# A decoder layer on one core: biases and beta added by accumulating transfers, the context's products in other accumulators, one product order, and the expert rows in another pool

## The chip, the cores and the metric

The kernel runs on one core of a Trainium2 chip. The metric is the device time of one execution in microseconds (us), lower being better. The core has five engines with a queue each, worked off in order: PE (TensorE, the matmuls; its weight loads, PEld, overlap them), DVE (VectorE), ACT (ScalarE), POOL (GpSimd) and SP (SyncE, which here only issues transfers). Transfers are issued from SP, ACT or POOL and share 16 DMA engines.

## What is computed

A decoder layer in float32, for x of 2 x 512 tokens by 1024 (E), that is 8 tiles of 128 tokens, and a context of 2 x 1024 by 1024:

```python
x = _layernorm(x + _L0_attn_ref(x, Wq, bq, Wk, bk, Wv, bv))       # per token, over head dims
x = _layernorm(x + _L0_xattn_ref(x, ctx, ...))                    # fake-quantised x @ fake-quantised ctx
x = _layernorm(x + _L0_ffn_ref(x, gate_w, up_w, down_w, fc1_w, fc2_w, expert_w, gamma, beta))
```

In the attention a token attends among its own 32 head dimensions: q (32 x 32), k and v (32 x 8) are projections with biases bq, bk, bv; the scores are a 32 x 32 matrix per token. The last part is relu(x up)^2 down, plus (x fc1) times the sum of the two largest gate logits, times expert and fc2, under a layer norm with gamma and beta.

## The kernel before

**Tiles and blocks.** Two tiles make a block of 256 tokens; there are four blocks. The tiles' own work is the generator `token_path` (L571): attention on DVE (`scores` L393, `exponentials` L412, `attend` L420), then the product with the quantised context (`cross` L527), then the hand-over (`hand_over` L617: transposes of the tile for the feed-forward, and `xc += beta` on POOL, L623, for the residual that is added at the very end, L774). The feed-forward of a block is the generator `ffn` (L649): 16 products with `up` (L695, PE name pu), 4 with `fc1` (pl), then `down` (L795, block 0, PE name pd) or `down_seven` (L851, blocks 1 to 3, PE name ps), which makes a product of 2 x 2 pieces with seven products in place of eight: per group of rows it needs sums of the activations (`unit_sums` L826) and of the weights (`weight_sums` L839, DVE L846 to L848).

**Order.** A loop at the end (L926 to L956) draws steps from the generators so that tiles of block n+1 are worked beside the feed-forward of block n. Before block 0, the generator `fill` (L334) runs beside tiles 0 and 1: it projects tiles 2 to 7 to q, k, v (L147, L152), copies them by ACT (L180, L181) and stores them to `qkv_d` in device memory from ACT's queue (L185, L186); then it multiplies expert and fc2 into four row blocks `e2` (L384, copies L388, stores L390 from POOL). The framework orders the instructions of each engine by an estimate of its own as it builds the program, within the dependencies; `tc.issue_after(i)` holds an instruction behind `i`.

**Biases.** bq (summed over four heads), bk and bv are spread to all partitions by a matmul and kept in `bqkv` (L213). Tiles 0 and 1 get the bias for q and k as they leave PSUM (L178). Later tiles are fetched back by `fetch_qkv` (L168, POOL's queue, L170 and L171) and get it on DVE (L189). The bias of v is added on DVE for every tile (L193).

**PSUM.** `ps_mm` has 2 banks (tag mm), for pu, pl, the context's products py (L559, L562) and pe; `ps_dn` has 4 (tag dn), for the projections and for pd and ps; `ps_tr` has 2. A py is taken out by DVE (L566), a pu by ACT (L722), a pl by DVE (L736).

**Seven products.** `order` (L883) is the order of the seven products of a group: (1, 2, 3, 6, 7, 5, 4), or (1, 6, 7, 5, 4, 2, 3) where the last three groups of the last block run together. Four banks hold them: 1 and 6, 2 and 3, 7 and 5, and 4. Products 1, 2, 3 read loaded weights as they are, 6 reads a sum that L847 writes over a part of them, 7 and 5 sums of L846, 4 a sum of L848. After the last group of each half (n = 0, 1) the banks are taken out: ACT L904 (1), DVE L905 (6), L906 (7), L907 and L908 (5), L909 (4), L912 (2 and 3). The weights come by `down_rows` (L753), 1 MB each, in three buffers (two of tag wb, one of tag wc).

**Pools.** `front` (L96) holds the projection weights, the x tiles (tag xs) and their transposes; the expert rows also take its xs buffers (L379). It is closed at L940, and the pools h, ffn, sums and more are opened in its place: the up activations, the relu buffers, the weight sums (and the loads of the second context, L477), one weight buffer. `work` has 3 buffers of 128 x 1024 for several short-lived rows.

Of the kernel before, what the change touches and what calls it, by code (L numbers as in the profile page):

```python
# [9 lines left out]
F32 = mybir.dt.float32  # L10
BF16 = mybir.dt.bfloat16
AF = mybir.ActivationFunctionType
ALU = mybir.AluOpType
# [3 lines left out]
P = 128  # L17
# [10 lines left out]
def kernel(  # L28
# [24 lines left out]
    nc = tc.nc  # L53

    B, S, E = x.shape
    _, D, H = wq.shape
    G = wk.shape[2]
    J = H // G
    DG = D * G
# [9 lines left out]
    TB = 2  # L69
    NB = TB * P  # L70
    NBLK = NT // TB
    HALF = 512
    DC = 8
# [39 lines left out]


    wqkv = [frontp.tile([P, 3 * DG], F32, name=f"wqkv_{k}") for k in range(KE)]
    bqkv = const.tile([P, 3 * DG], F32, name="bqkv")
    wq2 = wq.rearrange("e d h -> e (d h)")
    wk2 = wk.rearrange("e d h -> e (d h)")
    wv2 = wv.rearrange("e d h -> e (d h)")
# [54 lines left out]
    def projected(t, pqk, pv):  # L174

        qk, v = new_qkv(t, t >= TB)
        if t < TB:
            nc.vector.tensor_add(qk, pqk, bqkv[:, 0 : 2 * DG])  # L178
        else:
            nc.scalar.copy(qk, pqk)  # L180
        nc.scalar.copy(v.rearrange("p g e -> p e g"), pv[:, :DG].rearrange("p (e g) -> p e g", g=G))  # L181
        if t < TB:
            qkv[t] = qk, v
        else:
            nc.scalar.dma_start(qkv_d[t, :, 0 : 2 * DG], qk)  # L185
            nc.scalar.dma_start(qkv_d[t, :, 2 * DG :], v.rearrange("p g e -> p (g e)"))  # L186

    def bias_qk(qk):
        nc.vector.tensor_add(qk, qk, bqkv[:, 0 : 2 * DG])  # L189

    def bias_v(v):
        ve = v.rearrange("p g e -> p e g")
        nc.vector.tensor_add(  # L193
            ve, ve, bqkv[:, 2 * DG : 3 * DG].rearrange("p (e g) -> p e g", g=G)
        )


    brow = attp.tile([P, E], F32, tag="s", name="brow", bufs=2)
# [9 lines left out]
    for lo, n in ((0, 2 * DG), (2 * DG, DG)):  # L208
        pb = ps_mm.tile([P, HALF], F32, tag="mm", name=f"pb_{lo}")
        nc.tensor.matmul(  # L210
            pb[:, :n], ones_row[0:1, :], bqk_row[0:1, lo : lo + n], start=True, stop=True
        )
        nc.scalar.copy(bqkv[:, lo : lo + n], pb[:, :n])  # L213

# [62 lines left out]
    beta = const.tile([P, E], F32, name="beta")  # L277
# [55 lines left out]

    def fill():  # L334
        aside = context_tiles(0)
        xT = load_xT(TB)
        for t in range(TB, NT):
            for _ in range(2):
                next(aside, None)
            if t == NT - 3:  # L340
                nc.sync.dma_start(gamma, ln_gamma.partition_broadcast(P))
                nc.sync.dma_start(beta, ln_beta.partition_broadcast(P))
            ps = projection_psum(t)
            following = None
            for k in range(KE):
                project_qk(ps[0], xT, k)
                project_v(ps[1], xT, k)
                if k == 3:
                    yield 5.2
                if k == 4 and t + 1 < NT:  # L350

                    following = load_xT(t + 1)
                    yield 1.3
            xT = following
            projected(t, *ps)
            yield 5.2
        ex = wstream.tile([P, NL, LAT], F32, tag="wa", name="ex")
        nc.sync.dma_start(ex, expert_w.rearrange("(k p) n -> p k n", p=P))
        fc2 = []
        for c in range(NL // 2):  # L360
            w = wstream.tile([P, 2, E], F32, tag="wb", name=f"fc2_{c}")
            nc.sync.dma_start(w, fc2_w.rearrange("(k p) n -> p k n", p=P)[:, 2 * c : 2 * c + 2, :])
            fc2.append(w)
        expert = [None]
        exT = wstream.tile([P, NL, LAT], F32, tag="wa", name="exT")
        for m in range(NL):
            pt = ps_tr.tile([P, NL, P], F32, tag="tr", name=f"pt_ex_{m}")
            for l in range(NL):
                nc.tensor.transpose(pt[:, l, :], ex[:, l, ts(m, P)], ident)
            nc.scalar.copy(exT[:, m, :], pt.rearrange("p a b -> p (a b)"))  # L370
        yield 2.6
        for l in range(NL):

            while l >= NL // 2 and 1 not in crossed:
                yield 1.0
            if l == NL // 2:
                with tc.issue_after(expert[0].ins):
                    held.pop()()
            row = frontp.tile([P, E], F32, tag="xs", name=f"e2_{l}", bufs=2)  # L379
            for n in range(2):  # L380
                ps = ps_mm.tile([P, HALF], F32, tag="mm", name=f"pe2_{l}_{n}")
                with tc.issue_after(crossed[1].ins) if l >= NL // 2 else ExitStack():
                    for m in range(NL):
                        expert[0] = nc.tensor.matmul(  # L384
                            ps, exT[:, m, ts(l, P)], fc2[m // 2][:, m % 2, ts(n, HALF)],
                            start=(m == 0), stop=(m == NL - 1),
                        )
                nc.scalar.copy(row[:, ts(n, HALF)], ps)  # L388
                yield 3.5
            nc.gpsimd.dma_start(e2[ts(l, P), :], row)  # L390


    def scores(t, qk):  # L393
        q3 = qk[:, 0:DG].rearrange("p (d g) -> p d g", g=G)
        k3 = qk[:, DG : 2 * DG].rearrange("p (e g) -> p e g", g=G)
        s = attp.tile([P, D, D], F32, tag="s", name=f"s_{t}", bufs=2)
        for c in range(D // DC):
            prod = attp.tile([P, DC * D * G], F32, tag="prod", name=f"pqk_{t}_{c}", bufs=2)
            nc.vector.tensor_tensor(  # L399
                prod.rearrange("p (d e g) -> p d e g", d=DC, g=G),  # L400
                q3[:, ts(c, DC), :].unsqueeze(2).to_broadcast([P, DC, D, G]),
                k3.unsqueeze(1).to_broadcast([P, DC, D, G]),
                ALU.mult,
            )
# [122 lines left out]
    def cross(t, xc, cq, crow):  # L527
# [28 lines left out]
        nc.vector.tensor_mul(r, total, s12d2)  # L556
        nc.vector.scalar_tensor_tensor(xc, xc, r, crow, ALU.add, ALU.add)
        for h in range(E // HALF):
            py = ps_mm.tile([P, HALF], F32, tag="mm", name=f"py_{t}_{h}")  # L559
            with behind_products():  # L560
                for k in range(KC):
                    crossed[t] = nc.tensor.matmul(  # L562
                        py, aT[:, k, :], cq[:, k, ts(h, HALF)], start=(k == 0), stop=(k == KC - 1)
                    )
            xh = xc[:, ts(h, HALF)]
            nc.vector.scalar_tensor_tensor(xh, py, ns12, xh, ALU.mult, ALU.add)  # L566
# [4 lines left out]
    def token_path():  # L571
# [3 lines left out]
        for blk in range(NBLK):  # L575
            xcs = []
            x2T = []
            for i in range(TB):
# [5 lines left out]
                    fetch_qkv(t + 1)  # L584
                if t == TB:
                    first = last
                if t >= TB:

                    with tc.issue_after(first.ins):
                        bias_qk(qk)  # L590
                if ahead is None:
                    ahead = scores(t, qk)
                while True:
                    try:
                        step = next(ahead)
# [2 lines left out]
                        break  # L598
                    yield step
                exponentials(t, s)  # L600
                with tc.issue_after(first.ins) if t >= TB else ExitStack():
                    bias_v(v)
                yield 3.1
                ahead = None
                if t == 0:
# [11 lines left out]
                def hand_over(blk=blk, t=t, i=i, xc=xc, x2T=x2T):  # L617
                    if not x2T:
                        x2T.append(attp.tile([P, KE, NB], F32, tag="x2T", name=f"x2T_{blk}"))
                    with behind_products():  # L620
                        transpose_f32(x2T[0][:, :, ts(i, P)], xc, f"x2_{t}")

                    nc.gpsimd.tensor_tensor(xc, xc, beta, ALU.add)  # L623

# [226 lines left out]
    def down_seven(blk, h, units):  # L851
# [17 lines left out]
        while g < len(groups):  # L869
# [5 lines left out]
            if j == 0:  # L875
# [3 lines left out]
                    for i in range(4)  # L879
                ]  # L880
                banks = {1: b[0][:, 0], 6: b[0][:, 1], 2: b[1][:, 0], 3: b[1][:, 1],
                         7: b[2][:, 0], 5: b[2][:, 1], 4: b[3][:, 0]}
            order = (1, 6, 7, 5, 4, 2, 3) if along > 1 else (1, 2, 3, 6, 7, 5, 4)  # L883
            for m in order:
                for gg in range(g, g + along):
                    jj = groups[gg][1]
                    for k in range(2):
                        begins = jj == 0 and k == 0
                        second = begins and m in FIRST_OF

                        behind = began[FIRST_OF[m]] if second else above
                        with tc.issue_after(behind.ins) if begins else ExitStack():
                            began[m] = lately[0] = nc.tensor.matmul(  # L893
                                banks[m], units[jj][m][:, k, :], weights[gg][m][:, k, :],
                                start=begins and not second,
                                stop=(jj == len(h) - 1 and k == 1 and m not in FIRST_OF.values()),
                            )
# [92 lines left out]
```

## Time and profile before

| | |
|---|---|
| Median of 3 runs | 740.75 us (740.57, 740.75, 743.47) |
| The profiled execution's own time | 743.63 us |
| Its span, first to last instruction | 741.9 us |
| Mean granted TensorE clock | 0.989 |
| PE busy | 712.4 us (96%) |
| DVE busy | 576.4 us (78%) |
| ACT, POOL busy | 190.3 us (26%), 78.6 us (11%) |
| DMA | 122.70 MB, mean 165 GB/s |
| xc += beta on POOL (L623) | 8 x 2886 ns |
| bias adds on DVE (L189, L193) | 6 x 678 ns, 8 x 599 ns |

How to read it: busy time is the sum of an engine's instructions. The matmuls are pipelined, so a PE that shows busy may still start the next one late; the spacing of starts tells more. A row of the groups gives line, engine, operation, what is written from what, the shapes and the count, then busy time and mean of one, then the engine's idle time just before and what ended it. A row of the timeline gives start and length in us, engine, line, operation, and in brackets the idle time before it and what ended that. A table by stretches gives for each engine the busy time and, in brackets, its number of instructions, then the granted clock of PE, the busy share of the DMA engines and their GB/s.

### The profile page before, as it was taken

To read this page: it belongs to the slowest core of one execution; us is meant where nothing else is said; L and a number is where in the kernel's file an instruction comes from. 1 tells how busy PE (TensorE), PEld (TensorE's weight loads), DVE (VectorE), ACT (ScalarE), POOL (GpSimd) and SP (SyncE) were. 2 spreads that over 40 slices of the span, in tenths; PEclk is the share of its full clock that TensorE was granted. 3 is DMA by queue.
4 is the path that set the end of the run, shared out by engine and by line. 5 is a ranking of instruction groups with operands and counts; after the bars stand their busy time and mean duration, and the time that the engine had idled before them with its cause. 6 is when DMAs were issued, how large, how long until landed. Compare 5 with 4: busy or idle time off the path is not lost.

```text
span 741.9 us, 7731 instructions
## 1 busy us (share of the span) xinstructions
PE 712.4 (96%) x3076; PEld 537.8 (72%) x3076; DVE 576.4 (78%) x660; ACT 190.3 (26%) x308; POOL 78.6 (11%) x84
## 2 busy tenths in 40 slices
PE   6999999989999999999899999999999999999993
PEld 3666554468876444687688778887888888888882
DVE  4699997799999999999989999995437492013636
ACT  2097322222361214365140001243100012200001
POOL 2000002310101103120001020210100110000001
PEclk9999999999999999999899999999999999999997
DMA  7988103195535446574336444753554445445401
GB/s 277 346 308 318 64 22 113 57 328 172 160 114 178 142 157 234 191 249 126 108 113 191 150 134 150 232 166 113 173 174 164 164 148 174 138 170 172 169 1 57
DMA packets 74388, 122.70 MB, mean 165 GB/s; under 512 B 3104, under 2 KB 46880, under 8 KB 74352
## 3 DMA queue, kind: packets, MB, share of 16 engines
q1 hardware_dynamic: 68720, 107.49, 43.2%
q0 software_dynamic: 3616, 11.84, 4.5%
q10 hardware_dynamic: 2016, 2.88, 1.1%
q8 instruction: 24, 0.39, 0.2%
q14 instruction: 12, 0.10, 0.0%
HBM read 113.55 MB, written 8.65 MB: 165 GB/s over the span
## 4 chain that ended last, share of the span: by engine, by line
PE 50%; DVE 38%; issue 5%; DMA 3%; ACT 2%; POOL 2%; SPq 0%; POOLq 0%; ACTq 0%; DVEq 0%
PE ps L893 20%; PE pu L695 17%; DVE o L436 6%; DVE pqk L399 6%; DVE pav L430 6%; DVE s L405 5%; PE pl L695 5%; PE pqk L147 3%; PE py L562 2%; PE pe L384 2%; DVE stats L285 2%; POOL rstd L291 1%; DMA wq<-in_L_attn_Wq_dram 1%; DMA e<-e 1%; DVE tt L846 1%
## 5 line engine op out<-in xcount | busy, mean ns | idle before, releaser
L695 PE MATMUL pu<-x2T,up 128*128 128x256 f32 x1024 | 228.6, 384 | 5.5 <-DVE xc L566 2.9
L695 PEld LDWEIGHTS pu<-x2T,up 128*128 128x128 f32 x1024 | 195.5, 192 | 35.4 <-ACT relu L722 3.8
L846 DVE TENSOR_TENSOR tt<-dn 128x1024 f32<-128x1024 f32 x30 | 37.1, 1237 | 46.7 <-DMA dn<-in_L_ffn_down_w_dram 31.8
L399 DVE TENSOR_TENSOR pqk<-qk 128x2048 f32<-128x2048 f32 x32 | 72.5, 2280 | 0.0
L436 DVE TENSOR_REDUCE o<-pav 128x64 f32<-128x2048 f32 x32 | 72.4, 2273 | 0.0
L430 DVE TENSOR_TENSOR pav<-s,v 128x2048 f32<-128x2048 f32 x32 | 72.4, 2276 | 0.0
L405 DVE TENSOR_REDUCE s<-pqk 128x256 f32<-128x2048 f32 x32 | 72.4, 2277 | 0.0
L806 PE MATMUL pd<-dn,h 128*128 128x512 f32 x160 | 69.5, 593 | 0.0
L147 PE MATMUL pqk<-wqkv,xT 128*128 128x512 f32 x128 | 66.8, 622 | 1.0 <-DVE wqkv L224 0.7
L722 ACT ACTIVATE relu<-pu 128x256 f32<-128x256 f32 x64 | 24.3, 380 | 148.2 <-PE pu L695 139.6
L893 PE MATMUL ps<-tt,h 128*128 128x256 f32 x240 | 61.0, 379 | 0.0
L893 PE MATMUL ps<-dn,h 128*128 128x256 f32 x240 | 57.2, 380 | 1.6 <-DVE y L908 1.6
L893 PE MATMUL ps<-dn,s 128*128 128x256 f32 x240 | 56.5, 379 | 0.0
L806 PEld LDWEIGHTS pd<-dn,h 128*128 128x128 f32 x160 | 30.2, 190 | 36.1 <-issue 35.8
L695 PE MATMUL pl<-x2T,fc 128*128 128x256 f32 x256 | 55.9, 379 | 0.0
L291 POOL TENSOR_TENSOR rstd<-ve,neg_half 128x1 f32<-128x1 f32 x24 | 24.8, 1034 | 272.5 <-DVE ve L289 251.2
L695 PEld LDWEIGHTS pl<-x2T,fc 128*128 128x128 f32 x256 | 48.7, 190 | 6.5
L893 PEld LDWEIGHTS ps<-dn,h 128*128 128x128 f32 x240 | 45.1, 190 | 8.0 <-DVE y L908 2.0
L893 PEld LDWEIGHTS ps<-dn,s 128*128 128x128 f32 x240 | 45.7, 190 | 6.1
L893 PEld LDWEIGHTS ps<-tt,h 128*128 128x128 f32 x240 | 45.7, 190 | 6.1
L152 PEld LDWEIGHTS pv<-wqkv,xT 128*128 128x128 f32 x128 | 24.3, 190 | 24.2 <-issue 22.2
L904 ACT COPY y<-ps 128x256 f32<-128x256 f32 x6 | 2.2, 372 | 142.6 <-PE ps L893 142.6
(140 smaller groups left out, 784.0 us busy)
## 6 DMA issues: line engine op xcount, KB each, us to landing
dn<-in_L_ffn_down_w_dram SPq DMA_DIRECT2D x32, 1024.0 KB, 5.0
up<-in_L_ffn_up_w_dram SPq DMA_DIRECT2D x32, 1024.0 KB, 5.3
fc<-in_L_ffn_fc_w_dram SPq DMA_DIRECT2D x10, 1024.0 KB, 5.2
dn<-e SPq DMA_DIRECT2D x8, 1024.0 KB, 5.0
xs<-in_x_dram SPq DMA_DIRECT2D x8, 512.0 KB, 5.5
wq<-in_L_attn_Wq_dram SPq DMA_DIRECT2D x8, 512.0 KB, 6.7
xc<-in_x_dram SPq DMA_DIRECT2D x8, 512.0 KB, 5.7
ctx<-in_ctx_dram SPq DMA_DIRECT2D x8, 512.0 KB, 6.8
```

Of the source, the lines that this page charges most:

```text
L147: projecting[0] = nc.tensor.matmul(pqk, xT[:, k, :], wqkv[k][:, 0 : 2 * DG], start=(k == 0), stop=(k == KE - 1))
L152: nc.tensor.matmul(pv[:, :DG], xT[:, k, :], wqkv[k][:, 2 * DG : 3 * DG], start=(k == 0), stop=(k == KE - 1),)
L291: nc.gpsimd.tensor_tensor(rstd, ve, neg_half, ALU.pow)
L399: nc.vector.tensor_tensor(prod.rearrange("p (d e g) -> p d e g", d=DC, g=G), q3[:, ts(c, DC), :].unsqueeze(2).to_broadcast([P, DC, D, G]), ...
L405: nc.vector.tensor_reduce(s[:, ts(c, DC), :].rearrange("p d e -> p (d e)"), prod.rearrange("p (c g) -> p c g", g=G), AX.X, ALU.add,)
L430: nc.vector.tensor_tensor(prod.rearrange("p (d g e) -> p d g e", d=DC, g=G), s[:, ts(c, DC), :].unsqueeze(2).to_broadcast([P, DC, G, D]), ...
L436: nc.vector.tensor_reduce(o[:, ts(c, DC), :].rearrange("p d g -> p (d g)"), prod.rearrange("p (c e) -> p c e", e=D), AX.X, ALU.add,)
L695: lately[0] = nc.tensor.matmul(ps[:, :NB], ws[:, k, wcols], xT[:, k, :], start=(k == 0), stop=(k == KE - 1))
L722: nc.scalar.activation(r, ps, AF.Relu)
L806: lately[0] = nc.tensor.matmul(pd[i][n], h[kk // 4][:, i, kk % 4, :], w[:, k, ts(n, HALF)], start=(kk == 0), stop=(kk == NK - 1),)
L846: nc.vector.tensor_tensor(tt[:, 0:2], w[:, 1], w[:, :, 0], ALU.subtract)
L893: began[m] = lately[0] = nc.tensor.matmul(banks[m], units[jj][m][:, k, :], weights[gg][m][:, k, :], start=begins and not second, stop=(jj ...
```

## The change

Five edits.

1. `bqkv` becomes `bqk` and `bv_ge`, the latter in v's own layout. Before a later tile's q, k, v arrive, `lay_bias` writes the biases to its place in `qkv_d` from SP's queue (two transfers for each of tiles 2 to 7). `projected` then stores from POOL's queue with an accumulating transfer. The adds on DVE of tiles 2 to 7 go; tiles 0 and 1 keep theirs for v.
2. `xc += beta` becomes an accumulating transfer from POOL's queue.
3. A py goes to `ps_dn`, if its tile's block is after the first and the feed-forward of the block before has not yet come to its down product (`up_to`); otherwise to `ps_mm` as before.
4. The expert rows are taken from `work`.
5. The seven products always run in the order (1, 6, 7, 5, 4, 2, 3).

```diff
         else:
-            nc.scalar.dma_start(qkv_d[t, :, 0 : 2 * DG], qk)
-            nc.scalar.dma_start(qkv_d[t, :, 2 * DG :], v.rearrange("p g e -> p (g e)"))
-
-    def bias_qk(qk):
-        nc.vector.tensor_add(qk, qk, bqkv[:, 0 : 2 * DG])
-
-    def bias_v(v):
...
+            nc.gpsimd.dma_start(qkv_d[t, :, 0 : 2 * DG], qk, accum_op=ALU.add)
+            nc.gpsimd.dma_start(
+                qkv_d[t, :, 2 * DG :], v.rearrange("p g e -> p (g e)"), accum_op=ALU.add
+            )
+
+    def lay_bias(t):
+
+        nc.sync.dma_start(qkv_d[t, :, 0 : 2 * DG], bqk)
+        nc.sync.dma_start(qkv_d[t, :, 2 * DG :], bv_ge.rearrange("p g e -> p (g e)"))
...
         aside = context_tiles(0)
+        lay_bias(TB)
         xT = load_xT(TB)
...
                     following = load_xT(t + 1)
+                    lay_bias(t + 1)
...
-            row = frontp.tile([P, E], F32, tag="xs", name=f"e2_{l}", bufs=2)
+            row = work.tile([P, E], F32, tag="work", name=f"e2_{l}")
...
-            py = ps_mm.tile([P, HALF], F32, tag="mm", name=f"py_{t}_{h}")
+            if t < TB or up_to[0] >= t // TB:
+                py = ps_mm.tile([P, HALF], F32, tag="mm", name=f"py_{t}_{h}")
+            else:
+                py = ps_dn.tile([P, HALF], F32, tag="dn", name=f"py_{t}_{h}")
...
-                if t >= TB:
-
-                    with tc.issue_after(first.ins):
-                        bias_qk(qk)
                 if ahead is None:
-                    ahead = scores(t, qk)
+
+                    ahead = scores(t, qk, first if t >= TB else None)
...
-                with tc.issue_after(first.ins) if t >= TB else ExitStack():
-                    bias_v(v)
+                if t < TB:
+                    nc.vector.tensor_add(v, v, bv_ge)
...
-                    nc.gpsimd.tensor_tensor(xc, xc, beta, ALU.add)
+                    nc.gpsimd.dma_start(xc, beta, accum_op=ALU.add)
...
-            order = (1, 6, 7, 5, 4, 2, 3) if along > 1 else (1, 2, 3, 6, 7, 5, 4)
-            for m in order:
+            for m in (1, 6, 7, 5, 4, 2, 3):
```

`scores` holds the first operation of each of its pieces behind the given instruction, as the bias of q and k was held before.

More of the change, by code (lines that the diff above doesn't have):

```diff
@@ L115 @@
     wqkv = [frontp.tile([P, 3 * DG], F32, name=f"wqkv_{k}") for k in range(KE)]
-    bqkv = const.tile([P, 3 * DG], F32, name="bqkv")
+    bqk = const.tile([P, 2 * DG], F32, name="bqk")
+    bv_ge = const.tile([P, G, D], F32, name="bv_ge")
     wq2 = wq.rearrange("e d h -> e (d h)")
@@ L177, in projected @@
         if t < TB:
-            nc.vector.tensor_add(qk, pqk, bqkv[:, 0 : 2 * DG])
+            nc.vector.tensor_add(qk, pqk, bqk)
         else:
@@ L184, in projected @@
         else:
-            nc.scalar.dma_start(qkv_d[t, :, 0 : 2 * DG], qk)
-            nc.scalar.dma_start(qkv_d[t, :, 2 * DG :], v.rearrange("p g e -> p (g e)"))
-    def bias_qk(qk):
-        nc.vector.tensor_add(qk, qk, bqkv[:, 0 : 2 * DG])
-    def bias_v(v):
[L192 to L195, printed above, removed]
+            nc.gpsimd.dma_start(qkv_d[t, :, 0 : 2 * DG], qk, accum_op=ALU.add)
[5 more added lines that the diff above has]
+        nc.sync.dma_start(qkv_d[t, :, 2 * DG :], bv_ge.rearrange("p g e -> p (g e)"))
     brow = attp.tile([P, E], F32, tag="s", name="brow", bufs=2)
@@ L212 @@
         )
-        nc.scalar.copy(bqkv[:, lo : lo + n], pb[:, :n])
+        if lo == 0:
+            nc.scalar.copy(bqk, pb)
+        else:
+            nc.scalar.copy(
+                bv_ge.rearrange("p g e -> p e g"), pb[:, :n].rearrange("p (e g) -> p e g", g=G)
+            )
     qkv = {}
@@ L390, in fill, with scores @@
             nc.gpsimd.dma_start(e2[ts(l, P), :], row)
-    def scores(t, qk):
+    def scores(t, qk, behind=None):
         q3 = qk[:, 0:DG].rearrange("p (d g) -> p d g", g=G)
@@ L398, in scores @@
             prod = attp.tile([P, DC * D * G], F32, tag="prod", name=f"pqk_{t}_{c}", bufs=2)
[L399 to L404, printed above, removed]
+            with tc.issue_after(behind.ins) if behind is not None else ExitStack():
+                nc.vector.tensor_tensor(
+                    prod.rearrange("p (d e g) -> p d e g", d=DC, g=G),
+                    q3[:, ts(c, DC), :].unsqueeze(2).to_broadcast([P, DC, D, G]),
+                    k3.unsqueeze(1).to_broadcast([P, DC, D, G]),
+                    ALU.mult,
+                )
             nc.vector.tensor_reduce(
@@ L558, in cross @@
         for h in range(E // HALF):
-            py = ps_mm.tile([P, HALF], F32, tag="mm", name=f"py_{t}_{h}")
+            if t < TB or up_to[0] >= t // TB:
+                py = ps_mm.tile([P, HALF], F32, tag="mm", name=f"py_{t}_{h}")
+            else:
+                py = ps_dn.tile([P, HALF], F32, tag="dn", name=f"py_{t}_{h}")
             with behind_products():
```

## The prediction

> **What bounds the kernel now.** I read the page first: busy shares, then the chain.
>
> ```profile
> PE 712.4 (96%) x3076; PEld 537.8 (72%) x3076; DVE 576.4 (78%) x660; ACT 190.3 (26%) x308; POOL 78.6 (11%) x84
> ...
> PE 50%; DVE 38%; issue 5%; DMA 3%; ACT 2%; POOL 2%; SPq 0%; POOLq 0%; ACTq 0%; DVEq 0%
> ```
>
> The chain shares itself between PE and DVE, which would make every us saved on DVE worth 0.4. But the chain picks one of two engines that are both full, so I asked for PE's own waits from 140 us on (block 0's feed-forward begins at 150.5).
>
> ```profile
> PE pu L695 <- DVE xc L566: 2.9, 1, 2.9
> PE pu L695 <- ACT relu L722: 2.5, 2, 2.3
> PE ps L893 <- DVE y L908: 1.6, 1, 1.6
> PE pta L545 <- ACT a L537: 0.8, 1, 0.8
> ```
>
> That is everything: 7.8 us in 585. Start-to-start times agree: the 128x256 matmuls follow each other at 0.216 us, and from 20 to 140 us PE loses only some 4 us. So PE bounds the kernel between a start of about 18 us and a tail of about 17 us after the last matmul, and only what shortens these waits shortens it. The timeline and the table by stretches show the largest at its place:
>
> ```profile
> 358.12 3.62 PE L562 MATMUL py<-cq,aT 128*128 128x512 bf16 x16
> 361.57 0.38 PE L688 MATMUL pw<-ident,rwm 128*128 128x128 f32 x2
> 364.88 9.46 PE L695 MATMUL pu<-x2T,up 128*128 128x256 f32 x29 [2.92 <-DVE xc L566]
> ```
>
> ```profile
> 362.00:364.00 2.00, 0.00 (x0) 0.00 (x0) 2.00 (x1) 0.32 (x2) 0.00 (x0) 1.00 0.33 112
> 364.00:366.00 2.00, 1.12 (x3) 0.94 (x4) 2.00 (x3) 0.00 (x0) 0.00 (x0) 0.51 0.00 0
> 366.00:368.00 2.00, 2.00 (x6) 1.59 (x5) 2.00 (x3) 0.00 (x0) 0.00 (x0) 0.50 0.00 0
> 372.00:374.00 2.00, 2.00 (x11) 1.75 (x10) 2.00 (x4) 0.40 (x1) 0.00 (x0) 1.00 0.00 0
> ```
>
> Tile 4's two py hold both ps_mm banks until DVE reaches L566 at 364.07; PE idles 2.9 us, and then its granted clock is half: 6 matmuls per 2 us instead of 11. Some 14 matmuls at 0.43 instead of 0.216 us: another 3.0 us.
>
> **The clock, rule against row.** The Trainium skill ("TensorE: Matmul & The Clock Gate", Part 1) has the clock fall to half after an idle window of about 3.4 us. By it, 2.9 us idle should not do that, and removing the wait is worth 3.1 us (2.9 and the slower restart). By the row it did, and is worth 6.1 us, in this execution. The runs come in two groups, 740.57 and 740.75 against 743.47 and the profiled 743.63; the distance is 2.8 to 3.0 us, the price of the half clock. I infer that it falls in some executions only, not in the median one. So for the median I take 3.1.
>
> **Part 3, py in ps_dn.** No instruction is added. At 204 to 212 (tile 2), 358 (tile 4) and 507 (tile 6) the four dn banks are empty: the down product of the block before has been taken out, that of the own block starts at 389 at the earliest after 358, while L566 empties the py by 367.7. Tiles 3, 5, 7 fall into a down product and stay. In block 0 two pd stand early, at 211.55, and L566 frees tile 2's py at 212.84: 1.3 us, if PE has no pu to do first; it has 16, so I take 0. Gain 3.1 us (between 1.8 and 3.1; with the half clock 6.1).
>
> **Part 4, expert rows.** The relu buffers lie where `front` was, and it is not free until the last expert row is stored.
>
> ```profile
> 160.60 0.38 ACT L722 ACTIVATE relu<-pu 128x256 f32<-128x256 f32 x1 [8.55 <-DMA e<-e]
> 161.03 5.23 PE L695 MATMUL pu<-x2T,up 128*128 128x256 f32 x23 [2.32 <-ACT relu L722]
> ```
>
> The row's transfer starts at 151.53 and takes 9.0 us. With the rows in work, all else in front is done by 113. PE loses 2.5 us here, but the second up weight, issued at 150.70, lands in 8.1 us, at 158.8, and PE needs it from 158.5: 0.4 us stay at least. The DMA is at 0.97 to 1.04 busy there. The loads of the second context (3 x 0.5 MB at 161.3) also waited for front and may now come sooner: all inside this stretch they would cost up to 1.5 MB / 0.36 MB per us = 4.2 us, before 148 (share 0.10) nothing. So between +2.1 and -2.1 us; nearest to PE's own row I take +1.5. In work, four rows and q_t of tile 1 share 3 buffers; a row is made per 6.9 us and stored in 3.1: no wait. The 0.8 us wait at 204 (pta) needs ACT's a, itself after DVE; DVE is 3.2 us earlier by then (five bias adds), PE 1.5: I take +0.4.
>
> **Part 5, the order.** One of the changes from half 0 to half 1 stalls, in block 1:
>
> ```profile
> 420.20 1.13 PE L893 MATMUL ps<-dn,h 128*128 128x256 f32 x4
> ...
> 422.93 1.13 PE L893 MATMUL ps<-dn,h 128*128 128x256 f32 x4 [1.60 <-DVE y L908]
> 423.12 0.68 DVE L912 TENSOR_TENSOR y<-ps,y 128x512 f32<-128x512 f32 x1
> ```
>
> Product 2 of the new half waits for a bank that is emptied by L908. In the new order product 6 comes second, in the bank of product 1 that L905 has freed (419.73), and banks 1 and 6 of the last group are done 5 products (5 x 0.86 = 4.3 us) before its end, not 3. Gain 1.6 us (0 to 1.8). Two prices. Product 6 needs L847 0.86 us after its group's start instead of 2.6; in block 1, the tightest, L847 ends at 405.4 for the group at 407.64: 3.1 us to spare. And the raw weights are held until product 3, now last: the buffer is freed 2.6 us later (SP issues at 6.05 instead of 3.46 us into the group). Landing takes 5.0 us: a load issued at 407.85 instead of 405.25 lands at 412.85, L846 stood at 412.06. DVE waits 0.8 us; its group starts at 420.2, so PE does not.
>
> **Parts 1 and 2.** Removed from DVE: 6 x 0.678 (L189) and 6 x 0.599 (L193) = 7.7 us; the two v adds left may fall from 0.60 to the 0.42 of a contiguous 256. From POOL 8 x 2.886 = 23.1 us, and with it contention: while L623 ran at 389.76, a 128x1 operation of DVE (L556) took 2.22 us instead of 0.15. About 10 us less on DVE, but on PE's path nothing by itself: PE waits for DVE only as listed. It is the cover for parts 3 and 4: by 375 DVE is 7.1 us earlier (six L189, five L193), PE 5.0, so the emptying of pl by L736, in DVE's order, should not become PE's next wait. I charge 0.5 us for what an altered order costs (0 to 3).
>
> Added: on SP 12 issues, 12 x 0.4 = 4.8 us, and 2.4 MB written, in a stretch with the DMA at 0.87. They wait only for the bias copies (done at 10.8); x tiles and context loads queue behind. No x tile is waited for there; the last is issued at 68.26 and turned at 93.04, the last context tile is quantised at 77.5 and used at 88.3. 2.4 MB and as much read by the accumulation are 4.7 / 0.32 = 15 us of DMA, spread until 114, of which 75 to 115 stands at 0.10 to 0.14. Cost 0; without that cover some us.
>
> On POOL 20 accumulating issues. No row shows an accumulation. The nearest are POOL's plain transfers: issue 0.54 to 1.01 us, 512 KB landing in 3.1 (e2) to 6.2 us (ctx); one that also reads its target moves twice the bytes, so 3 to 18 us. beta's are not needed before L774, 25 us later at least; q, k, v not before 140, after tile 2's store at 51. Against moving the stores from ACT to POOL speaks the Trainium skill ("SBUF — State Buffer", "Summary: rules for kernel authors"): hide a transfer under DVE work by issuing it from ACT or SP, since POOL's making of descriptors is starved by DVE's fast modes. By the rule each issue could wait out a DVE operation, 20 x 2.28 = 46 us; by the row 20 x 0.6 = 12 us, beside DVE at 99%. Either lies on an engine 11% busy and loses 23 us elsewhere. I take the row, and 0 on the path. What counts is the queue: each store waits for ACT's copy and the laid bias, and behind it stand fetches and rstd (L291).
>
> **Sum.** 3.1 + 1.5 + 0.4 + 1.6 - 0.5 = 6.1 us. Median: 740.75 - 6.1 = 734.6. From the profiled execution: 743.63 - 6.1 - 3.0 = 734.5 (a span near 732.8).
>
> **Rivals.** (a) *Likeliest, 0.62*: as summed, 731.5 to 737.5. (b) *The waits move, 0.20*: the second context's loads keep PE waiting at 158, PE runs ahead of DVE and waits for L736 or a weight sum. For: DVE is 96 to 100% busy from 162 to 460. Against: its 10 us. Only parts 3 and 5 by half: 740.75 - 2.3 = 738.4. (c) *Slower, 0.10*: POOL's order puts the store of tile 6 ahead of tile 0's first rstd. That rstd is at 90.97; tile 6's v is copied at 99.84, and two issues of 1.0 follow: rstd at 101.9, 10.9 us late. DVE takes L297 in order behind it, so the front, where DVE is 99% busy, grows by as much: 740.75 - 6.1 + 10.9 = 745.5. It decides from any store whose copy ends after 90.5; those of tiles 2 to 5 (done by 84) cost nothing. Against: the order estimate must be out by 9 us. (d) *DVE was the bound, 0.08*: all 10 us saved on it come through beside PE's 1.6 at 420: 740.75 - 11.6 = 729.1. For: 38% of the chain. Against: the list of PE's waits. That the change leaves ps_mm full is contained in (b).
>
> **The numbers.** A measurement of this kernel tells about 0.5% (3.7 us) from no change: faster is below 737.05, slower above 744.45. (a) gives 0.60 faster and 0.02 same, (d) 0.08 faster, (b) 0.20 same, (c) 0.10 slower: 0.68, 0.22, 0.10. The range leaves out (c) and half of (d): 730 to 741.
>
> **What would show it.** Right: PE has no wait for L566 near 360 and no half clock there; py of tiles 2, 4, 6 stand beside pu without a gap; L722 no longer waits for a row's transfer; no wait of ps for L908; DVE busy falls by some 10 us to about 566, POOL's to about 67. Wrong: a new row in PE's waits after 140, above all for L736, L847 or an up transfer; rstd of tile 0 after 95; first pg later than 151; or a PE idle of 3 us with a half clock behind it, anywhere.

## The result, and the profile after

| | before | after |
|---|---|---|
| Median | 741.75 us (16 runs, 740.44 to 743.67) | 739.25 us (16 runs, 737.87 to 740.34) |
| Ratio to before, 95% interval | | 0.9964 [0.9954, 0.9974] |
| A second set of runs | 741.83 us (32 runs) | 737.90 us (5 runs), 0.9953 [0.9937, 0.9970] |
| Profiled execution, its span | 743.63, 741.9 us | 738.42, 736.7 us |

The three runs of before that are shown ahead are among its sixteen. The change gains 2.5 us in the first set and 3.9 in the second; forecast were 6.1. The page of the changed kernel:

```profile
PE 708.9 (96%) x3076; PEld 535.4 (73%) x3076; DVE 565.3 (77%) x648; ACT 189.2 (26%) x308; POOL 66.7 (9%) x96
```

DVE's 565.3 and POOL's 66.7 us are the 566 and 67 that the prediction named: the work moved as said. PE's waits from 140 us on:

```profile
PE pu L704 <- DMA up<-in_L_ffn_up_w_dram: 3.8, 2, 2.2
PE pt_x L129 <- DVE xc L302: 1.0, 1, 1.0
PE pta L553 <- ACT a L545: 0.2, 1, 0.2
```

Three of the four rows that were to go are gone (py's emptying, relu, ps). In their place stand an up transfer, twice (at 159 and 325), and a hand-over that waits for DVE (at 431). The places at which before lost most, now:

```profile
358.64 3.62 PE L574 MATMUL py<-cq,aT 128*128 128x512 bf16 x16
362.09 0.38 PE L697 MATMUL pw<-ident,rwm 128*128 128x128 f32 x2
362.31 4.05 PE L704 MATMUL pu<-x2T,up 128*128 128x256 f32 x18
```

No gap after py. But 36 us earlier stands a new one, with a half clock behind it (the timeline of PE, then the table by stretches):

```profile
317.78 5.34 PE L704 MATMUL pu<-x2T,up 128*128 128x256 f32 x24
325.29 6.89 PE L704 MATMUL pu<-x2T,up 128*128 128x256 f32 x23 [2.17 <-DMA up<-in_L_ffn_up_w_dram]
```

```profile
324.00:326.00 2.00, 0.71 (x3) 0.68 (x4) 2.00 (x5) 2.00 (x2) 0.00 (x0) 1.00 0.98 259
326.00:328.00 2.00, 2.00 (x7) 1.61 (x6) 2.00 (x2) 0.16 (x1) 0.00 (x0) 0.57 1.08 371
328.00:330.00 2.00, 2.00 (x7) 1.62 (x6) 1.54 (x5) 0.00 (x0) 0.87 (x1) 0.58 0.29 101
330.00:332.00 2.00, 2.00 (x11) 1.76 (x10) 2.00 (x3) 2.00 (x3) 0.00 (x0) 1.00 0.00 0
```

Why the weight is late is in SP's timeline, first of before, then of after. A row with x2 holds two issues; the second one is at 318.40 in before and at 323.15 in after.

```profile
311.49 7.27 SPq L718 DMA_DIRECT2D up<-in_L_ffn_up_w_dram  x2
322.63 0.34 SPq L581 DMA_DIRECT2D xc<-in_x_dram  x1
```

```profile
309.14 0.43 SPq L727 DMA_DIRECT2D up<-in_L_ffn_up_w_dram  x1
316.63 0.34 SPq L593 DMA_DIRECT2D xc<-in_x_dram  x1
317.03 6.49 SPq L727 DMA_DIRECT2D up<-in_L_ffn_up_w_dram  x2
```

PE waits for the fourth up weight of block 1, issued at 318.40 in before and at 317.03 now. The load of tile 5's x, which waits for DVE (L783 starts at 315.33), stood behind that weight's load and now stands ahead of it. No edit asks for that: the framework ordered SP's queue anew.

The order is only half of the delay. The up weights have two buffers, so a load can go out only when PE has finished the weight before last, and PE then needs it some 7.2 us later (316.45 to 323.61 in x5_from_pool below, where x does not stand ahead). In before this load had no room either: it landed at 325.54, and PE used it at 325.67. By the spacing in x5_from_pool I estimate that the load went out 1.2 us late in the change; the other 1.1 of the 2.3 us that PE loses come from its landing, which took 8.1 us (7.1 in before, 6.4 in x5_from_pool).

The end of the program is longer too. POOL ends with a long instruction that the trace calls a drain. The profile's rows leave drains out; the trace's records of POOL have them:

```
                 POOL's transfers   its last drain   last store landed to the end
before           38                 3.76 us          1.10 us
after            58                 5.40 us          2.21 us
```

From the last matmul on, before takes 12.8 us and after 13.9.

### The profile page after: what moved, and what is told of

Its sections match the earlier page's. It is cut to its first block, busy times and chain, and to the rows that moved or that the text cites. A ratio compares the mean times of both kernels' runs of the same rounds, so it can differ in the third digit from the quotient of the medians.

```text
span 736.7 us, 7748 instructions
## 1 busy us (share of the span) xinstructions
PE 708.9 (96%) x3076; PEld 535.4 (73%) x3076; DVE 565.3 (77%) x648; ACT 189.2 (26%) x308; POOL 66.7 (9%) x96
## 5 line engine op out<-in xcount | busy, mean ns | idle before, releaser
L901 PE MATMUL ps<-dn,h 128*128 128x256 f32 x240 | 61.1, 380 | 0.0
L901 PE MATMUL ps<-dn,s 128*128 128x256 f32 x240 | 60.9, 379 | 0.0
L296 POOL TENSOR_TENSOR rstd<-ve,neg_half 128x1 f32<-128x1 f32 x24 | 19.7, 820 | 223.7 <-DVE ve L294 202.0
L153 PE MATMUL pv<-wqkv,xT 128*128 128x256 f32 x128 | 35.7, 379 | 0.0
```

The lines of the kernel that those rows point to most:

```text
L153: nc.tensor.matmul(pv[:, :DG], xT[:, k, :], wqkv[k][:, 2 * DG : 3 * DG], start=(k == 0), stop=(k == KE - 1),)
L296: nc.gpsimd.tensor_tensor(rstd, ve, neg_half, ALU.pow)
L901: began[m] = lately[0] = nc.tensor.matmul(banks[m], units[jj][m][:, k, :], weights[gg][m][:, k, :], start=begins and not second, stop=(jj ...
```

## Experiments

Two stretches are used below: from the first gate product (pg, some 150 us) to tile 5's hand-over (pt_x, some 430 us), called *the stretch* (288.6 us before, 282.1 after), and from there to the end. In the change the hand-over stands six products (1.3 us) earlier in PE's order, so 1.3 of the stretch's 6.5 us are no gain. "Lost" is the time between two starts of PE over the usual spacing.

**One edit undone at a time.** First theory: the gains came, and the late up load took them back. Against it: DVE's relief is what gained; or the added traffic costs.

```diff
undo1 (edit 1)
-            nc.gpsimd.dma_start(qkv_d[t, :, 0 : 2 * DG], qk, accum_op=ALU.add)
+            nc.scalar.dma_start(qkv_d[t, :, 0 : 2 * DG], qk)
...
+                        bias_qk(qk)
undo2 (edit 2)
-                    nc.gpsimd.dma_start(xc, beta, accum_op=ALU.add)
+                    nc.gpsimd.tensor_tensor(xc, xc, beta, ALU.add)
undo3 (edit 3)
-                py = ps_dn.tile([P, HALF], F32, tag="dn", name=f"py_{t}_{h}")
+            py = ps_mm.tile([P, HALF], F32, tag="mm", name=f"py_{t}_{h}")
undo4 (edit 4)
-            row = work.tile([P, E], F32, tag="work", name=f"e2_{l}")
+            row = frontp.tile([P, E], F32, tag="xs", name=f"e2_{l}", bufs=2)
undo5 (edit 5)
-            for m in (1, 6, 7, 5, 4, 2, 3):
+            order = (1, 6, 7, 5, 4, 2, 3) if along > 1 else (1, 2, 3, 6, 7, 5, 4)
```

> The changed kernel with edit 1 undone: biases again by bqkv, plain stores from ACT, bias adds on DVE. Theory (the gains came, a new wait near 322 us took them back): here the load of tile 5's x stands behind the third and fourth up load of block 1 in SP's queue, so PE's wait for an up transfer near 322 (2.2 us, and the half clock behind it, some 1.7) is gone; 735.5 to 737 against 739.25 of the change. Rival 1 (DVE's relief is what gained): 7.7 us of adds come back to DVE, 741 or more. Rival 2 (the added traffic of the accumulating stores costs it back): the first pg comes at least 1.5 us before 149.3, and the time falls by as much, 737 to 738, with no change near 322.

> The changed kernel with edit 2 undone: beta is added by POOL again. Theory: the load of tile 5's x stands behind the up loads again, no wait for an up transfer near 322: 735.5 to 737. POOL gets 23 us of work back and slows DVE's small operations beside it by some 2 us each, which PE should not see. Rival 1 (DVE's relief gained): the contention returns, 740 to 742. Rival 2 (traffic): 3.4 MB less in all but nothing less in the front, so the first pg stays at 149.3 and the time within 0.5 us of 739.25.

> The changed kernel with edit 3 undone: all py in ps_mm. Theory: PE's wait near 322 is gone by the queue's order (some 3.9 us back), but the wait for the taking out of py near 360 returns (2.9 us, and up to 3 with the half clock): about 738 to 741.5, near the change. Rival 1: DVE has the same work as in the change, so 739.25 within 0.5. Rival 2: also within 0.5 of 739.25, first pg at 149.3.

> The changed kernel with edit 4 undone: the expert rows in front's buffers. Theory: the wait near 322 stays (2.2 us and half clock), the wait near 160 for relu, 2.3 us, returns in place of 1.8 for the second up weight, which it hides: 0.5 to 1.5 us slower than the change, 739.7 to 740.7. Rival (edit 4 costs time, since the loads of the second context now come at 113 in the full front): up to 1.5 us faster, and the first pg before 149.

> The changed kernel with edit 5 undone: the old product order outside the last groups. Theory: the wait near 322 stays, the wait of ps for L908 in block 1 (1.6 us) may return: 739.5 to 741. Rival (the order costs, since the raw weights are held 2.6 us longer in every group): faster than the change by 0.5 or more, 738.7 or less.

| | median us | ratio to before [95%] |
|---|---|---|
| undo1 | 738.77 | 0.9959 [0.9947, 0.9972] |
| undo2 | 740.57 | 0.9985 [0.9976, 0.9993] |
| undo3 | 737.85 | 0.9947 [0.9926, 0.9967] |
| undo4 | 740.06 | 0.9987 [0.9970, 1.0003] |
| undo5 | 739.69 | 0.9973 [0.9962, 0.9984] |
| the change | 739.25 | 0.9964 [0.9954, 0.9974] |

Only edit 2's undoing has an interval clear of the change's (1.3 us slower by the medians). Undoing edit 3, to which I had given the most, shows no loss at all. In undo1 and undo2 PE's wait near 322 is gone, as expected, but neither reaches the 735.5 to 737 us of the first theory. undo2 lies where the rival, DVE's relief, had it (740 to 742). In its profile DVE is 4.7 us busier than in the change (570.0 against 565.3), and PE loses 3.9 us at relu (198 and 333) and pta (202), where activations stand behind a tile's quantising; whether POOL's additions beside DVE or the new order cause that is not settled. Each of the five places PE's waits elsewhere; undo3 has the old one back, but no half clock with it:

```profile
PE pu L700 <- DVE xc L574: 2.1, 1, 2.1
PE ps L897 <- DVE y L912: 0.7, 1, 0.7
PE pt_x L129 <- DVE xc L302: 0.6, 1, 0.6
```

**Edits in pairs.**

```diff
only35, only12, no35: the kernel before with edits 3 and 5; with 1 and 2; with 1, 2 and 4
(as in the change's diff)
```

> The kernel before with edits 3 and 5 alone: py in ps_dn and the product order. Theory: PE's waits for L566 and L908 go and the load of tile 5's x stays behind the up loads: 741.75 - 3.1 to 6.1 - 1.6 = 734 to 737. Rival 1 (the gain of the change comes from DVE's relief by edits 1 and 2): within 1 us of the kernel before, 740.7 to 742.7.

> The kernel before with edits 1 and 2 alone (biases and beta by accumulating transfers). Theory D (DVE bounds the stretch from the first gate product at 150 us to the hand-over of tile 5 at 430 to 439, PE's waits in it are slack; the end of the kernel pays 0.082 us for each transfer that POOL issued): the stretch shortens from 288.6 by the DVE work taken out of it, 6 to 7 us, as in the change (282.1), though all PE's waits of before stay; the end, from the last matmul on, is 13.9 as in the change; 738 to 740.5, so the change's gain or nearly. Theory P (PE's waits bound, and the change's gain came from taking those of py, relu and ps away): the stretch stays within 2 us of 288.6, 741 to 743.

> The kernel before with edits 1, 2 and 4, so the changed kernel without both edits that take waits of PE away. Theory D: these two gain nothing, 737.5 to 739.5, with PE's waits for the taking out of py (2 us) and for ps standing, and the stretch within 1 us of 282.1. Theory P: their 4.7 us are missing, 742 or more. Theory O (each build is ordered anew, and what decides is which load or activation comes to stand behind a waiting one, as in only12, where it cost 6 us near 487): neither number, and the difference stands in one wait of PE that the change doesn't have.

only35: 746.37 us, 1.0060 [1.0042, 1.0078]. only12: 747.10, 1.0060 [1.0040, 1.0079]. no35: 741.88, 1.0000 [0.9986, 1.0014]. Both pairs are slower than before by some 4.5 us (0.60%), which nobody expected, and no35 gains nothing. Beside the change, timed with it (737.90), no35 is 4.0 us slower. That is near what I forecast for edits 3 and 5 together (3.1 + 1.6), though neither undone alone costs it, and in part by luck: in no35's profile 2.7 us are back at py and 1.7 at ps, but 2.9 more are lost behind ACT's relu steps at 481 and 490, where the change loses at most 0.5. only35 loses 2.7 us at 378, where PE waits for DVE to take out a pl (L740, L736 of before), 2.3 at 480 for an up weight, and 2.3 with a half clock of 3.4 us at 167 for another. Where only12 loses its time, ACT's timeline shows, and beside it the table by stretches:

```profile
480.62 0.42 ACT L728 ACTIVATE h<-relu 128x256 f32<-128x256 f32 x1
487.36 1.24 ACT L317 ACTIVATE qt<-xc,z,rs 128x1024 f32<-128x1024 f32 x1 [6.32 <-DVE xc L302]
488.63 1.15 ACT L320 ACTIVATE qt<-qt,round_up 128x1024 f32<-128x1024 f32 x1
489.69 0.36 ACT L727 ACTIVATE relu<-pu 128x256 f32<-128x256 f32 x1
```

```profile
488.00:490.00 2.00, 0.00 (x0) 0.00 (x0) 2.00 (x2) 1.97 (x4) 0.00 (x0) 0.81 0.82 225
490.00:492.00 2.00, 1.90 (x5) 1.53 (x6) 2.00 (x4) 2.00 (x4) 0.00 (x0) 0.50 0.87 300
492.00:494.00 2.00, 2.00 (x6) 1.62 (x5) 2.00 (x3) 1.21 (x4) 0.00 (x0) 0.50 0.00 0
494.00:496.00 2.00, 2.00 (x6) 1.53 (x6) 2.00 (x2) 0.00 (x0) 0.00 (x0) 0.50 0.00 0
```

A tile's quantising stands ahead of relu on ACT and waits 6.3 us for DVE; PE, which needs relu to empty ps_mm, loses 3.2 us, and then 3.0 more at half clock. no35 has the same order there (ACT waits 6.1 us, PE loses 1.9, the clock holds). From the first gate product to the last matmul the two profiles differ by 4.4 us (580.1 and 575.6), and that place makes 4.3 of it; edit 4, the only difference between the two kernels, acts 330 us earlier.

**The late up load, taken away.**

```diff
x5_from_pool
-                nc.sync.dma_start(xc, xf[ts(t, P), :])
+                (nc.gpsimd if t == 5 else nc.sync).dma_start(xc, xf[ts(t, P), :])
dn_held (the down weights of block 0 behind the third up load)
+        with tc.issue_after(third[0].ins) if name.count("_") == 2 else ExitStack():
             nc.sync.dma_start(w, src[:, :, n0 : n0 + nn])
```

> The changed kernel with one transfer moved: the load of tile 5's x is issued from POOL's queue and not from SP's, so that the up loads behind it do not wait for DVE's last step of the tile before. Theory: PE's wait for an up transfer near 322 and the half clock to 330 are gone, 3 to 4 us: 735.3 to 736.3. Rivals 1 and 2: the wait near 322 is hidden behind something else that is late (DVE, or the transfers): within 1 us of 739.25.

> The changed kernel with the three loads of block 0's down weights held in SP's queue behind the third up load. Theory: the second up weight no longer shares the DMA engines with two loads of 1 MB; it lands before PE asks for it at 157, the wait of 1.8 us there goes: 737.2 to 738.2. Rival (the up load waits for its buffer or for the expert row and context transfers, not for the down loads): wait of 1 to 2 us stays, within 0.5 of 739.25; and where the down weights come late for block 0's own down product near 211, slower by up to 3 us.

x5_from_pool: 739.04 us, 0.9961 [0.9949, 0.9972]; dn_held: 738.62, 0.9958 [0.9946, 0.9970]. Both do at their place what they were to do (no wait at 322 in the one, none at 157 in the other), and neither gains what that was worth. dn_held loses 2.4 us near 325 and 2.0 at 417 instead. In x5_from_pool the stretch is 281.9 us: PE comes earlier to the next place at which it depends on a tile, and waits there.

```profile
330.66 1.24 ACT L317 ACTIVATE qt<-xc,z,rs 128x1024 f32<-128x1024 f32 x1 [3.84 <-DVE xc L302]
331.81 0.36 ACT L731 ACTIVATE relu<-pu 128x256 f32<-128x256 f32 x1
```

It loses 1.7 us here, 0.7 and 0.9 at 401 and 416, 1.2 at 430. So the first theory falls as far as it said that this one wait costs 4 us of the time.

**Is it DVE after all?** In the stretch DVE is idle for only 8.2 us of 282. New theory D: DVE bounds it. dve_less leaves out one product of the scores per tile, dve_more does one of their sums twice.

```diff
dve_less (in scores; tiles 2 to 5)
+                2 <= t <= 5 and c == 1 or nc.vector.tensor_tensor(
dve_more
+            ) for _ in range(2 if 2 <= t <= 5 and c == 1 else 1)]
```

> The changed kernel without one product of 2.27 us on DVE in each of tiles 2 to 5 (the second quarter of the scores' products is left out and the first one reduced twice): 9.1 us less on DVE between 150 and 430, nothing else. Theory D: the stretch from the first gate product to tile 5's hand-over falls below 282.1 until PE's own work of 276 us bounds it, so by 4 to 6 us: 733.5 to 735.5. Theory P: DVE's load is not on the path, within 1 us of 739.25.

> The changed kernel with one sum of 2.27 us on DVE done twice in each of tiles 2 to 5: 9.1 us more on DVE between 150 and 430, nothing else. Theory D (DVE bounds the stretch): 282.1 grows by 8 to 9 us, 747 to 748.5. Theory P (PE bounds, DVE has slack): it grows by 3 us at most, below 742.5. Between: both are full and share it, 743 to 746.

dve_less: 738.39 us, 0.9938 [0.9918, 0.9958]. dve_more: 738.81, 0.9961 [0.9948, 0.9975].

```profile
PE 707.4 (96%) x3066; PEld 533.8 (73%) x3076; DVE 573.2 (78%) x652; ACT 189.8 (26%) x308; POOL 66.2 (9%) x96
```

DVE has 8 us more than in the change (573.2 against 565.3), and the stretch takes 282.6 us instead of 282.1; with 8 us less (557.3) it takes 280.0, without the half clock that cost the change 1.7 us. Theory D, which asked for 8 to 9 us more and 4 to 6 less, falls. Of the added 8 us, 4.4 lie in the stretch and 3.5 behind it: DVE is full there because it works ahead on later tiles, and it lets that work slip (its last product of scores in the front starts at 440.7 instead of 434.5) when it has more to do.

**The next wait, taken away too.** In x5_from_pool, tile 4's quantising is held behind the last activation that had been issued:

```diff
both_couplings
-            for _ in below_top(tmp, xc, tmp, rs1, z1):
-                pass
+            with tc.issue_after(acted[0].ins) if t == 4 else ExitStack():
+                list(below_top(tmp, xc, tmp, rs1, z1))
```

> The kernel of x5_from_pool, and the quantising of tile 4 held on ACT behind the last activation that the program had issued by then. In x5_from_pool PE's wait at 322 was gone, and 1.7 us of PE's waiting came back at 330: there relu stood on ACT behind tile 4's quantising, which waited 3.8 us for DVE. PE's order is the same as in x5_from_pool. Theory W (PE bounds the stretch; a wait taken away lets PE run into the next instruction that stands behind tile work on an in-order queue): with this one away too, no wait at 330, and the stretch from the first gate product to tile 5's hand-over is 280 to 280.5 instead of 281.9, the time 737.2 to 738. Theory D' (PE meets DVE's pace before 430 in any case): the 1.7 us come back at 401 to 430 as longer waits, stretch 281.5 or more, time within 0.5 us of x5_from_pool's 739.04.

739.43 us, 0.9968 [0.9956, 0.9981]: no gain. The wait at 330 is gone. But the up weight issued at 316.33 landed 8.7 us later in this profile (PE resumes at 325.18), where x5_from_pool, issuing at 316.45, had it in 6.4 us and did not wait:

```profile
316.50 7.15 PE L704 MATMUL pu<-x2T,up 128*128 128x256 f32 x32
325.18 2.18 PE L704 MATMUL pu<-x2T,up 128*128 128x256 f32 x9 [1.52 <-DMA up<-in_L_ffn_up_w_dram]
```

The stretch is 281.7 us. As a landing decided this profile, it does not tell the two theories apart; the timed runs say only that the two edits bring less than 1 us together.

**The end.**

```diff
pool20 (60 in pool60), in the kernel before
...
+                        [nc.gpsimd.dma_start(spare[0:1, n : n + 1], ln_beta[n : n + 1].unsqueeze(0)) for n in range(20 if t == NT - 1 else 0)]
no3_fewer_pool: undo3, and the gate weights and the four expert rows from ACT's queue
...
-            nc.gpsimd.dma_start(e2[ts(l, P), :], row)
+            nc.scalar.dma_start(e2[ts(l, P), :], row)
```

> The kernel before with 20 transfers of 4 bytes added on POOL's queue behind the last addition of beta, read by nobody: as many issues on POOL as the change adds. Theory of the end: POOL's last drain takes 0.082 us for each transfer that POOL has issued, 5.4 us instead of 3.76, and ends 1.1 us later than the last store lands; the stretch from the last matmul to the end is 13.9 instead of 12.8, and the time 742.5 to 743.2, 1.1 over before. Rival (the end was longer by the accumulating transfers themselves, or by chance): 12.8 and within 0.5 us of before.

> As pool20, with 60 transfers of 4 bytes, so 98 issues on POOL. By the profile (0.082 us each): POOL's last drain takes 8.7 us instead of 3.76 and ends 4.4 us after the last store has landed; if the timed executions pay for it as the profiled one does, 746 to 746.5. If the long drain is of profiled executions alone: 741.7 to 742.7. pool20 left that open, with 1.1 us in its profile and a ratio of 1.0002 [0.999, 1.0013].

> The changed kernel without edit 3 (737.85 when it ran alone), and with five of POOL's transfers, the gate weights and the four expert rows, issued from ACT's queue. Theory of the end: 5 x 0.082 = 0.4 us less in POOL's last drain, 737.0 to 738.0. Rival: the stores of the expert rows hold ACT up, or the front: 738 or more.

```
                 POOL's transfers   its last drain   last matmul to the end   median us   ratio to before [95%]
pool20           58                 5.40 us          13.9 us                  742.51      1.0002 [0.9990, 1.0013]
pool60           98                 8.66 us          17.2 us                  745.89      1.0056 [1.0035, 1.0077]
no3_fewer_pool   53                 4.98 us          13.5 us                  738.78      0.9950 [0.9934, 0.9965]
```

38, 53, 58 and 98 transfers give 3.76, 4.98, 5.40 and 8.66 us: 0.082 us for each. In pool20's time the 1.1 us do not show (0.2 us, its interval ends at 1.0); pool60 is 3.9 us slower, where its profile has 4.4. So by its profile the change pays 1.1 us at its end for 20 more transfers on POOL. no3_fewer_pool shows its 0.4 us in the profile, and in the time nothing beyond undo3.

**Both kernels once more.**

```diff
before_again, after_again: no edit
```

> The kernel before once more, for a second profile of it. If the profile shown was typical: first gate product at 149 to 151.5, PE's wait of 2.9 us near 362 with a half clock behind it, 288 to 289 us from the first gate product to tile 5's hand-over, 12.8 us from the last matmul to the end. If the half clock was of that execution alone, as the prediction had it: none near 362, and the stretch 3 us shorter.

> The changed kernel once more, for a second profile of it. If the profile shown was typical: the wait for an up transfer near 322 and a half clock behind it, 281.5 to 283 us from the first gate product to tile 5's hand-over, 13.9 us from the last matmul to the end. If the wait near 322 was chance, the stretch is 4 us shorter.

741.73 us, 1.0004 [0.9991, 1.0017], and 737.90, 0.9953 [0.9937, 0.9970]. The second profile of before has PE's waits again, and a half clock again, of 3.4 us instead of 6.8:

```profile
PE pu L695 <- DVE xc L566: 2.9, 1, 2.9
PE pu L695 <- ACT relu L722: 2.8, 2, 2.6
PE ps L893 <- DVE y L908: 1.6, 1, 1.6
PE pta L545 <- ACT a L537: 0.8, 1, 0.8
```

```profile
362.00:364.00 2.00, 0.61 (x2) 0.55 (x3) 2.00 (x3) 0.00 (x0) 0.00 (x0) 0.92 0.01 1
364.00:366.00 2.00, 2.00 (x6) 1.56 (x6) 2.00 (x2) 0.00 (x0) 0.00 (x0) 0.50 0.00 0
366.00:368.00 2.00, 2.00 (x9) 1.67 (x8) 2.00 (x6) 0.00 (x0) 0.00 (x0) 0.73 0.00 0
```

The second profile of after has the wait near 322 (1.7 us), without a half clock.

## Why the prediction was wrong, step by step

The sums close. From the first gate product to the last matmul, before takes 578.5 and 577.5 us in its two profiles, after 573.5 and 573.3. What PE loses from 140 us on, half clock included, is 12.0 and 10.6 us before, 7.3 and 6.3 after (gaps over 0.35 us): 4.7 and 4.3 less, where the whole falls by 5.0 and 4.2. With 1.1 more at the end, and a first gate product that lies at 149 to 151 in both, 3.1 to 3.9 us are left, beside 2.5 and 3.9 in the timed runs.

- *What bounds.* "PE bounds the kernel ... only what shortens these waits shortens it" stands: the sums say so, and 8 us more or less on DVE move the medians by less than 1 us (each beside its own runs of before, by 1.9 at most). Rival (d), DVE, is refuted. The 17 us given for the tail behind the last matmul are 12.8; no term rests on them.
- *Part 3*, 3.1 us: right at its place, and too low. The wait is gone, and with it a half clock that was in all four profiles of before's order (before, its repeat, pool20, pool60), worth 1.7 us where it lasted 3.4 us and 3.0 where it lasted 6.8. I had taken it out of the median, by the rule of the Trainium skill ("TensorE: Matmul & The Clock Gate", Part 1: an idle window of some 3.4 us), and since the first three runs looked like two groups. Sixteen runs fill the range from 740.44 to 743.67 with no gap over 0.6, and 2.9 us of idle were enough in each profile: the row was right, not the rule. The timed runs agree: of the 134 of before beside the experiments, 104 have a mean clock below 0.992 and a median of 742.1 us, the other 30 one of 740.6. As half clock at the end counts into that mean, I only infer from it that most executions have the half clock here, the median one too.
- *Part 4*, 1.5 us: 2.5 and 2.7 us lost there became 1.8 and 0.7, so 0.7 and 2.0: near the forecast, though the up weight that I gave 0.4 us cost 1.8 in the first profile; in dn_held, where block 0's down weights load behind it, this wait is gone.
- *pta*, 0.4: 0.9 became 0.4. As forecast.
- *Part 5*, 1.6: the 1.8 us at 421 are gone in the first profile of after; in the second, 0.7 and 0.9 stand at 401 and 416 instead.
- *The altered order* is the step that failed: "I charge 0.5 us for what an altered order costs (0 to 3)". At places where before loses nothing, PE lost 5.2 us in the first profile (at 322 2.3 and the half clock 1.7, at 430 1.1) and 3.5 in the second (1.9 at 323, 1.2 at 430, 0.5 at 480). I had followed each queue past which an instruction was moved by the edits, but took the rest of the order for fixed. It is not: the load of tile 5's x changed its place in SP's queue though no edit touches it, and the hand-over of tile 5 moved six products (1.3 us) up in PE's order, where it meets DVE's work on that tile 1.1 us too early. Not all of it is order: at 322, 1.1 us (0.6 in the second profile) are the weight's landing, and so are the 0.5 at 480. I had also not asked how long an up weight has to land: some 7.2 us, with none to spare near 322 even in before.
- *Parts 1 and 2*, 0 on the path: DVE's relief is worth less than 1 us by the medians of dve_less and dve_more (undo2 leaves open whether POOL's additions beside DVE cost 1.3), but the end is not free. The prediction counted 20 issues on POOL at 0.6 us and did not ask what POOL does with them when the program closes: 1.1 us.

So 1.7 us that I had left out were gained; 3 to 4.7 beyond my charge went to the new places, some to part 5, and 1.1 to the end. What happened is nearest to rival (b), and its waits appear in part: the one at 158 stays (1.8 and 0.7 us), and a weight sum costs 0.7 us in the second profile. The wait for L736, which (b) names too, costs nothing in the change, but 2.7 us in only35, which lacks DVE's relief (and 1.4 in dve_less, which has more of it, so that DVE's load alone does not decide it). The forecast of 734.6 us was 4.65 us too low.

Open: why PE loses 4.7 to 10.0 us in gaps of the stretch in every one of the 20 profiles, wherever the order puts them. Taking one wait away brought the next, and the last try was decided by a landing. So that the order was the cause is read from the traces; no run undid the new order alone and got the time back.

## What to carry to other kernels

Where a framework orders the queues anew at each build, an edit's gain isn't its own: two pairs of these edits cost 4.5 us each, and the five together gain 2.5 to 3.9. Before summing removed waits, list for each in-order queue what stands behind an instruction that waits for another engine, compare the time that each buffered load has with the time it takes to land, and leave room for a wait of 2 to 4 us, half clock included, to reappear. An engine that is busy to 97% over a stretch, as DVE here, need not be the bound: give it more work on purpose, and see.

## What the hardware showed

- POOL's drain at the end of the program took 0.082 us for each transfer issued from POOL in the whole program (38 to 98 transfers, 3.76 to 8.66 us). In before it ended 0.2 us before the last store landed (740.53 against 740.75) and cost nothing. In undo1, with 46 transfers, it ended 0.4 us after, and the end came 0.1 us later than in before; from there on each transfer counts in full.
- In the 20 profiles, each of the six times from 140 us on that two matmuls started 3.13 to 3.41 us apart was followed by half clock, 3 of 11 from 2.33 to 3.02 us, and none of 20 from 1.71 to 2.30. The half clock lasted 3.4 us, at a price of 1.7, or 6.8 us, at a price of 3.0 (before, only12) or 3.1 (undo4).
- The same load of 1 MB, of the up weight that PE needs near 323.5, took between 5.2 and 8.7 us to land in the 20 profiles; the median of all up weights is 5.2 to 5.4. In the change and its repeat it took 8.1 and 7.6 us. In both_couplings and x5_from_pool it was issued at the same time to 0.1 us and took 8.7 and 6.4. It has some 7.2 us, so whether PE waits there depends on the landing as well as on the order.
